# A four-layer graph network: nodes dealt to partitions in fours, adjacency alone on GpSimd's queue, and other work moved off GpSimd

**Chip, cores, metric.** One core of one Trainium2 chip. The metric is the device time of a run in microseconds (us); lower is better.

## The reference, cut to what matters

`x` is 8 x 2048 x 64, `adj` is 2048 x 2048 (random, symmetric in its zeros, each row scaled to sum 1). Every layer is pre-normed and added to `x`:

```python
# --- layer 0 (adj_preln) ---
h = jnp.maximum(_layernorm(x, axis=-1), 0.0)
x = x + _L0_gnn_ref(h, adj, embedding, weight, bias)    # h, A h, 2 A A h - h; weights per node
# --- layer 1 ---
h = jnp.maximum(_layernorm(x, axis=-1), 0.0)
x = x + _L1_gnn_ref(h, adj, ...)                        # three steps, each with one adj @ v
# --- layer 2 ---
h = jnp.maximum(_layernorm(x, axis=-1), 0.0)
x = x + _L2_gnn_ref(h, adj, ...)                        # one adj @ x
# --- layer 3 ---
h = jnp.maximum(_layernorm(x, axis=-1), 0.0)
x = x + _L3_gnn_ref(h, adj, a)                          # attention
return x
```

## The kernel before

The kernel keeps the signs of the whole adjacency on chip (`BT`, 8 MB as fp32) and scales the sums of each product by a row factor (`crow`). In the prologue, TensorE forms seven of the eight first products while the sixteen adjacency chunks arrive; the eighth (its line is L494 before; below "the 7th bank is done" means the start of it) reuses a bank. Batches go in four pairs `p`, nodes in four blocks `nb` of 512. A float32 value is split into two parts, `H` (a rounded copy by ScalarE) and `L` (the rest, by VectorE), and each part is multiplied.

Names in the lines below: Pool is GpSimd's short name in the profile. `bv_..a` and `bv_..b` are layer 0's first and second products; in layer 0 `y` is the product with the per-node weights and `odd` half of its sums on VectorE; `ph` belongs to layer 1, `e` is layer 2's product, `pS` and the other `y` are layer 3's sums and the row made of them. `h` is the normed `x`, `hb` a block of it that was stored and is loaded again. `MD` is the copy of the transposed signs in the chip's large memory (DRAM).

The places that the change and the argument touch:

```python
def fill_x(acc, layer, p, nb, queue=nc.sync):           # x of one block: runs of 64 floats, 256 B
    if layer == 0:
        for bb in range(2):
            ld = queue.dma_start(
                acc[:, :, bb * C:(bb + 1) * C],
                x[2 * p + bb].rearrange("(j p) c -> p j c", p=P)[:, part(nb), :],
            )
        return ld
# ... (cut)
def load_adj(m):                                        # one chunk: 128 rows of 8 KB, on Pool's queue
    loads.append(nc.gpsimd.dma_start(BT[:, m, :], adj[m * P:(m + 1) * P, :]))
# ... prologue: Pool issues chunks of adj between loads of x (lx) and powers (cut)
pool_loads(order[0], ((row, 0), (lx, 2), (row, 1), (lx, 3), (row, 2)))
plan = {
    0: (0, ((lx, 4),)), 1: (1, ((row, 3), (lx, 5), (row, 4))),
    2: (2, ((lx, 6), (row, 5), (lx, 7))), 3: (3, ((row, 6), (row, 7), (dia, 0), (dia, 1))),
    # ... (cut)
}
# ... layer 0, after each block's sums (cut)
nc.vector.tensor_tensor(acc, acc, odd, op=ALU.add)
keep(p, nb, acc, f"1_{p}_{nb}")     # starts the norm, stores the sums to xs (Pool queue);
                                    # the store of h (Pool queue) follows when the norm is done
# ... then, in the block loop (cut)
with tc.issue_after(kept[-1].ins):
    m = 4 * p + nb
    nc.gpsimd.dma_start(MD[m * P:(m + 1) * P, :], BTf[:, m, :])   # fp32 -> bf16 on the way
# ... layer 1, last step (cut)
acc = load_x(1, p, nb)
nc.gpsimd.tensor_tensor(acc, acc, rows4(b2r), op=ALU.add)
pn = back_to_nodes(g_new[nb], w2T, nm)
nc.vector.tensor_tensor(acc, pn, acc, op=ALU.add)
# ... layer 3, the end (cut)
for nb in range(NB):
    acc = accs[NB * p + nb]
    (nc.gpsimd if nb == 0 else nc.vector).tensor_tensor(acc, acc, rows4(y), op=ALU.add)
    queue = (nc.gpsimd, nc.sync, nc.scalar, nc.sync)[nb] if p == NP - 1 else nc.sync
    for bb in range(2):
        queue.dma_start(
            out[2 * p + bb].rearrange("(j p) c -> p j c", p=P)[:, part(nb), :],
            acc[:, :, bb * C:(bb + 1) * C],
        )
```

## Time and profile before

| kernel before | value |
|---|---|
| median of three runs | 1280.3 us (1279.38 to 1283.99) |
| span of the profiled run | 1278.6 us |
| TensorE busy | 1217.3 us, 95% |
| first matmul | 15.1 us |
| 7th bank done (first matmul of L494) | 81.5 us |
| last `y` of layer 3 (start of its making; behind it only adds and stores) | 1261.9 us |
| from there to the end of the span | 16.8 us |

### The profile page before, as it was taken

The numbers are of one execution on the slowest core, as the hardware profiler recorded it, in microseconds if no ns is written. First come the engines' busy times: TensorE is split into PE (matmuls) and PEld (weight loads), VectorE is DVE, ScalarE is ACT, GpSimd is POOL, SyncE is SP. The second block draws the span as 40 slices with busy tenths as digits, with TensorE's granted clock in tenths as the row PEclk, the third lists the DMA queues.
The fourth block names the chain that finished last, engine by engine and source line by source line (L and its number), as shares of the span: only waits on it lengthen the run. The fifth ranks groups of instructions, "written<-read, shape, count | busy, mean of one in ns | idle before, by whom it ended". The sixth has DMA issues, their size and how long they took to land.

```text
span 1278.6 us, 15515 instructions
## 1 busy us (share of the span) xinstructions
PE 1217.3 (95%) x5702; PEld 862.7 (67%) x5702; DVE 751.4 (59%) x1936; ACT 182.3 (14%) x281; POOL 236.8 (19%) x244
## 2 busy tenths in 40 slices
PE   4899999999999999999999999999999999999993
PEld 3665554555575556755567888787788787788882
DVE  5445887767746776377654446445543554575653
ACT  5530010000010000000011121112111111211100
POOL 6410211111121111011110024004102400432222
PEclk9999999999999999999999999999999999999996
DMA  8982343323332222122255425433643543524321
GB/s 265 343 208 74 96 112 87 90 70 84 95 105 71 71 79 66 65 62 62 67 141 136 102 93 158 112 92 121 150 117 87 159 116 86 161 95 115 108 58 36
DMA packets 140057, 141.14 MB, mean 110 GB/s; under 512 B 95093, under 2 KB 97141, under 8 KB 137925
## 3 DMA queue, kind: packets, MB, share of 16 engines
q1 hardware_dynamic: 121092, 82.05, 25.2%
q0 software_dynamic: 12160, 49.10, 12.8%
q10 hardware_dynamic: 6720, 8.92, 2.5%
q8 instruction: 47, 0.77, 0.2%
q14 instruction: 38, 0.30, 0.1%
HBM read 95.92 MB, written 35.73 MB: 103 GB/s over the span
## 4 chain that ended last, share of the span: by engine, by line
PE 83%; DMA 6%; DVE 4%; issue 3%; POOL 2%; ACT 1%; SPq 0%; ACTq 0%; POOLq 0%; DVEq 0%
PE bv L222 34%; PE y L632 23%; PE bn L587 4%; PE ph L804 3%; PE bv_0b L222 2%; PE bv_2b L222 2%; DMA BT<-in_adj_dram 2%; PE bv_3b L222 2%; PE bv_1b L222 2%; DMA hb<-hs 1%; POOL rstd L170 1%; PE bv_0a L222 1%; PE bv_3a L222 1%; PE bv_2a L222 1%; PE bv_1a L222 1%
## 5 line engine op out<-in xcount | busy, mean ns | idle before, releaser
L222 PE MATMUL bv<-BT,H 128*128 128x512 f32 x1024 | 426.7, 417 | 0.0
L222 PE MATMUL bv<-BT,L 128*128 128x512 f32 x1024 | 401.2, 392 | 0.0
L222 PEld LDWEIGHTS bv<-BT,H 128*128 128x128 f32 x1024 | 192.6, 188 | 47.9 <-issue 11.6
L222 PEld LDWEIGHTS bv<-BT,L 128*128 128x128 f32 x1024 | 192.9, 188 | 47.3 <-issue 11.5
L641 DVE SCALAR_TENSOR_TENSOR acc<-y,emb,acc 128x128 f32<-128x128 f32 x512 | 176.2, 344 | 65.8 <-PE y L632 62.4
L632 PE MATMUL y<-wt,t0T 64*128 64x512 f32 x512 | 144.2, 608 | 10.0 <-DVE odd L641 10.0
L641 DVE SCALAR_TENSOR_TENSOR odd<-y,emb,odd 128x128 f32<-128x128 f32 x448 | 153.3, 342 | 0.0
L170 POOL TENSOR_TENSOR rstd<-var,mhalf 128x8 f32<-128x8 f32 x64 | 107.9, 1688 | 194.5 <-DVE var L168 184.3
L214 DVE TENSOR_TENSOR g<-bv,crow 128x512 f32<-128x512 f32 x48 | 33.2, 691 | 183.7 <-PE bv L222 183.7
L164 ACT ACTIVATE sq<-z 128x512 f32<-128x512 f32 x64 | 40.4, 631 | 406.5 <-DVE z L160 397.4
L632 PEld LDWEIGHTS y<-wt,t0T 64*128 64x128 f32 x512 | 46.7, 187 | 73.9 <-issue 68.0
L612 POOL TENSOR_TENSOR acc<-acc,wl 128x512 f32<-128x512 f32 x16 | 20.6, 1289 | 297.3 <-DVE z L160 297.2
L613 POOL DMA_DIRECT2D xs<-acc x32 | 18.0, 562 | 276.2 <-DVE acc L649 254.2
L632 PE MATMUL y<-wt,t1T 64*128 64x512 f32 x256 | 67.9, 596 | 0.0
L173 DVE SCALAR_TENSOR_TENSOR z<-z,rstd 128x512 f32<-128x512 f32 x64 | 45.9, 723 | 28.2 <-POOL rstd L170 28.2
L587 PEld LDWEIGHTS bn<-wl,g 128*128 128x128 f32 x384 | 49.5, 191 | 6.3 <-ACT H L206 1.6
L167 DVE TENSOR_REDUCE var<-sq 128x8 f32<-128x512 f32 x64 | 43.5, 679 | 15.8 <-ACT sq L164 15.8
L587 PE MATMUL bn<-wl,g 128*128 128x128 f32 x384 | 51.1, 276 | 1.0 <-DVE var L168 0.5
L749 DVE SCALAR_TENSOR_TENSOR junk<-mt,cols,st 128x512 uint8<-128x512 bf16 x64 | 50.8, 794 | 0.6
L632 PEld LDWEIGHTS y<-wt,t1T 64*128 64x128 f32 x256 | 27.7, 188 | 27.3 <-issue 27.3
L809 ACT ACTIVATE g<-g,b1s 128x512 f32<-128x512 f32 x32 | 23.2, 724 | 139.4 <-DVE g L808 139.3
L160 DVE TENSOR_TENSOR z<-acc,mean 128x512 f32<-128x512 f32 x56 | 38.3, 690 | 6.6 <-DMA hs<-z 5.2
(209 smaller groups left out, 1677.3 us busy)
## 6 DMA issues: line engine op xcount, KB each, us to landing
BT<-in_adj_dram POOLq DMA_DIRECT2D x16, 1024.0 KB, 9.2
crow<-crowD SPq DMA_DIRECT2D x64, 256.0 KB, 3.2
st<-in_adj_dram SPq DMA_DIRECT2D x64, 256.0 KB, 3.4
hs<-z POOLq DMA_DIRECT2D x40, 256.0 KB, 2.8
xs<-acc POOLq DMA_DIRECT2D x32, 256.0 KB, 2.5
MD<-BT POOLq DMA_DIRECT2D x16, 512.0 KB, 5.0
acc<-xs SPq DMA_DIRECT2D x32, 256.0 KB, 3.2
hb<-hs SPq DMA_DIRECT2D x28, 256.0 KB, 3.6
```

What stands on the lines that cost most here:

```text
L160: firsts.append(nc.vector.tensor_tensor(g, groups(xt), mean[:, :, None].to_broadcast([P, 8, C]), op=ALU.subtract))
L164: squares.append(nc.scalar.activation(sq, z, AF.Square))
L167: nc.vector.tensor_reduce(var, groups(sq), axis=AX.X, op=ALU.add)
L170: powers.append(nc.gpsimd.tensor_tensor(rstd, var, mhalf, op=ALU.pow))
L173: nc.vector.scalar_tensor_tensor(groups(h), g, 0.0, rstd[:, :, None].to_broadcast([P, 8, C]), op0=ALU.max, op1=ALU.mult)
L214: ahead.append(nc.vector.tensor_tensor(out, ps, crow, op=ALU.mult))
L222: nc.tensor.matmul(ps, hl[m // 4][i][:, m % 4, :], BT[:, m, nb * 512:(nb + 1) * 512], start=(m == 0 and i == 0), stop=(m == NCH - 1 and i ...
L587: nc.tensor.matmul(ps[:, t, :], fT[:, t * P:(t + 1) * P], wmat, start=True, stop=True)
L632: nc.tensor.matmul(y[:, bb, :], terms[k][hs_, ts], wt[hs_, k, dg * 512:(dg + 1) * 512], start=(k == 0), stop=(k == K - 1),)
L641: last = nc.vector.scalar_tensor_tensor(xj, yd, ec, old, op0=ALU.mult, op1=ALU.add)
L749: nc.vector.scalar_tensor_tensor(junk, mt, cols[:, i, :], st, op0=ALU.mult, op1=ALU.not_equal, accum_out=bad[:, i, q:q + 1],)
L804: fill[12] = lambda: nc.tensor.matmul(ph, w1v2 if s else w1vT, gT[nb], start=True, stop=True)
```

## The change

Its intent: (1) a chunk of 128 rows holds every fourth node of a block, so that four neighbouring nodes lie in one partition and `x`, the embedding and the result move in runs of 1 KB instead of 256 B; (2) in the prologue `x` comes on SyncE's queue alone, Pool issues nothing but the adjacency, seven chunks at once, and ScalarE stores `h`; (3) the sums, whose columns are now nodes in another order, are read from PSUM in steps of four; (4) the constant `b2` is added in layer 0 instead of layer 1; (5) at the end all four adds are on VectorE and no store on Pool. The arithmetic is the same.

```diff
+    def rows_of(a, m):
+        return a.rearrange("(b p t) n -> b t p n", p=P, t=4)[m // 4, m % 4]
+    def runs_of(a, p, nb):
+        return a[2 * p:2 * p + 2].rearrange("e (b p t) c -> b p e (t c)", p=P, t=4)[nb]
 # fill_x
-            for bb in range(2):
-                ld = queue.dma_start(acc[:, :, bb * C:(bb + 1) * C], ...)      # cut
+            return queue.dma_start(runs(acc), runs_of(x, p, nb))
 # scaled (the sums)
-        ahead.append(nc.vector.tensor_tensor(out, ps, crow, op=ALU.mult))
+        crow, to = (a.rearrange("p (t q) -> p t q", t=4) for a in (crow, out))
+        ahead.append(nc.vector.tensor_tensor(
+            to, ps.rearrange("p (q t) -> p t q", t=4), crow, op=ALU.mult
+        ))
 # prologue
-    load_x01(nc.scalar)
-    load_x01()
+    for _ in norm_order:
+        load_x01(nc.sync)
-    pool_loads(order[0], ((row, 0), (lx, 2), (row, 1), (lx, 3), (row, 2)))
+    pool_loads(order[0], tuple((row, m) for m in range(7)))
+        1: (1, ((row, 7), (row, 8))), 2: (2, ((row, 9), (row, 10))),           # plan, cut
-        if m in (13, 14):                                                      # crow products
+        if m > 13:
-                for nb in (0, 1) if m == 13 else (2, 3):
+                for nb in (0, 1) if m == 14 else (2, 3):
 # layer 0 (keep) and layer 1
-        if more is not None:
-            nc.gpsimd.tensor_tensor(acc, acc, more, op=ALU.add)
+        nc.gpsimd.tensor_tensor(nodes(acc), nodes(acc), more, op=ALU.add)
-        keep(p, nb, acc, f"1_{p}_{nb}")
+        keep(p, nb, acc, f"1_{p}_{nb}", b2r[:, None, None].to_broadcast([P, 4, 2, C]))
-                    nc.gpsimd.tensor_tensor(acc, acc, rows4(b2r), op=ALU.add)
 # the end
-            (nc.gpsimd if nb == 0 else nc.vector).tensor_tensor(acc, acc, rows4(y), op=ALU.add)
-            queue = (nc.gpsimd, nc.sync, nc.scalar, nc.sync)[nb] if p == NP - 1 else nc.sync
+            nc.vector.tensor_tensor(nodes(acc), nodes(acc), rows4(y), op=ALU.add)
+            queue = nc.scalar if nb % 2 == 0 and p == NP - 1 else nc.sync
+            queue.dma_start(runs_of(out, p, nb), runs(acc))
 # cut: the prologue's stages of the norm in a stricter order, weight loads, embedding, diagonal
```

## The prediction

> **What bounds the kernel now.** I read first the page's busy shares and its 40 slices, then the table of stretches, the waits of the first 95 us, the order of work on Pool there, and the last 20 us in order of time.
>
> ```profile
> PE 1217.3 (95%) x5702; PEld 862.7 (67%) x5702; DVE 751.4 (59%) x1936; ACT 182.3 (14%) x281; POOL 236.8 (19%) x244
> ...
> PE   4899999999999999999999999999999999999993
> ...
> DMA  8982343323332222122255425433643543524321
> ```
>
> TensorE is full from the third slice to the last but one, so only the two ends can give much. The DMA row is high only in the first two slices. The table of stretches (stretch: length, PE, PEld, DVE, ACT, POOL busy, clock, DMA share, GB/s) confirms it:
>
> ```profile
> 0.00:10.00 10.00, 0.00 (x0) 0.00 (x0) 2.18 (x5) 1.72 (x2) 5.51 (x14) 1.00 0.87 261
> 10.00:20.00 10.00, 4.88 (x12) 3.83 (x13) 8.18 (x19) 7.97 (x11) 6.98 (x8) 1.00 0.88 266
> ...
> 30.00:40.00 10.00, 7.14 (x22) 4.92 (x23) 4.98 (x12) 4.55 (x6) 7.38 (x8) 0.85 0.92 308
> ...
> 60.00:70.00 10.00, 9.05 (x38) 6.68 (x37) 2.20 (x16) 6.13 (x7) 0.00 (x0) 1.00 1.28 416
> ...
> 300.00:700.00 400.00, 395.61 (x1807) 246.85 (x1804) 258.52 (x796) 32.82 (x55) 47.63 (x55) 1.00 0.32 83
> 700.00:1000.00 300.00, 299.00 (x1453) 240.81 (x1452) 143.25 (x265) 53.31 (x88) 53.93 (x50) 1.00 0.44 116
> ```
>
> From 300 to 1000 us TensorE lacks 5.4 of 700 us. The prologue moves 261 to 308 GB/s for 40 us, though the same engines reach 416 when only the adjacency is in flight. What waits there, in us in total, times, longest:
>
> ```profile
> PE bv_0a L418 <- ACT H L206: 15.1, 1, 15.1
> PE bv_0a L418 <- ACT BT L319: 4.5, 4, 1.9
> ...
> ACT BT L319 <- DMA BT<-in_adj_dram: 18.3, 10, 4.0
> ```
>
> The first matmul comes at 15.12 us, and afterwards the signs (and TensorE behind them) wait for adjacency rows. The rows come late because Pool issues them between other things. Its order of work (start, length, what):
>
> ```profile
> 5.90 0.59 POOL L305 DMA_DIRECT2D BT<-in_adj_dram  x1
> 12.02 3.29 POOL L170 TENSOR_TENSOR rstd<-var,mhalf 128x8 f32<-128x8 f32 x2 [5.53 <-DVE var L168]
> 15.27 1.55 POOL L126 DMA_DIRECT2D x<-in_x_dram  x2
> 16.81 0.57 POOL L305 DMA_DIRECT2D BT<-in_adj_dram  x1
> ```
>
> Three rows are out by 6.5 us and the fourth only at 16.8. The trace's single DMA packets show the hole: between 15.4 and 18.4 us no 8 KB adjacency packet starts at all.
>
> The end, in order of time:
>
> ```profile
> 1263.16 1.76 POOL L870 TENSOR_TENSOR acc<-acc,y 128x512 f32<-128x512 f32 x1 [4.19 <-DVE y L867]
> 1265.22 1.57 POOL L873 DMA_DIRECT2D out_dram<-acc  x2 [0.29 <-POOL acc L870]
> 1265.40 0.68 DVE L870 TENSOR_TENSOR acc<-acc,y 128x512 f32<-128x512 f32 x1
> ...
> 1266.11 1.24 SPq L873 DMA_DIRECT2D out_dram<-acc  x2
> ```
>
> The last store is issued by 1267.4, yet the span ends at 1278.6. The trace's raw records tell why: Pool waits until its own two stores have landed (1270.41), runs a semaphore step of 1.54 us, then a DRAIN of 5.62 us (1272.16 to 1277.78), and the other engines, done by 1273.4, wait for it.
>
> **What the Trainium skill says.** "DMA: Bandwidth & Descriptors", section Queues, rings and completion order: a DMA engine alternates between its queues at packet granularity. The trace agrees: with both queues full, from 4.5 to 5.5 us, 36 packets of 8 KB start beside 20 of 256 B, so a small packet waits for about one large one. The same page, Latency and other measured facts, has a large loss at row pitches of 512 KB and more; the new adjacency pitch is 32 KB, which no run here shows. "SBUF — State Buffer", Who interferes with whom: a VectorE instruction with two SBUF inputs and a GpSimd one that reads SBUF block each other. The trace agrees: the VectorE add beside Pool's took 1.75 us and the next 0.68. The same page, section Door 1, gives PSUM 8-byte lines and a penalty for broken access (stated for matmuls); no instruction before reads PSUM in steps, so this is open.
>
> **The change, part by part.**
>
> (1) Start. x now goes alone on SyncE, in 1 KB runs, one DMA per block. The first block used 1024 packets of 256 B on the ScalarE queue and was read at 7.92 us, its last packets stuck between adjacency packets. SyncE's first packets start at 1.9 us and Pool's at 3.7. Estimate: 16 packets of 1 KB per engine at about 0.055 us (the 2 KB h stores took 0.095) is 0.9 us, so two blocks pass before the adjacency starts; the first is usable near 4.5, 3.4 us sooner. The same chain of norm, power and copy then puts the first matmul at 11.5 instead of 15.1.
>
> (2) Stream. Seven rows are issued at once and the rest well ahead, so the DMA engines should never run dry. Work per engine: 128 adjacency packets at 0.35 us (between 0.328, alone, and 0.38, the mean) = 44.8; x, 93 packets left at 0.055 = 5.1; the diagonal, 16 of 4 KB at 0.2 = 3.2; h, 64 of 2 KB at 0.095 = 6.1. Sum 59.2, from 3.7: the last row ends near 63 where it ended at 70.5. Does x starve, alternating one to one? A round is about 0.42 us; 93 rounds put the eighth block at 44 us, and it is first needed with row 13, near 52. A pair of x blocks lasts four rows, and in 32 rounds exactly four rows arrive. It fits.
>
> (3) End of the prologue. The pass is 224 matmuls at 0.227 us = 50.9, plus some 2.4 for the slow clock of the first 5 us (0.43 per matmul) and 2.0 for the crow transposes: 55.3. From 11.5 that gives 66.8 as TensorE's floor. The DMA side gives 63 + 1 (landing) + 1 (half a sign) + 20 matmuls (4.5) + 1 = 70.5. The crow products move one row later, so the sums are scaled later and the next product may wait 1 us for its bank: 71.5, against 81.4 for the first matmul of L494 before. **Gain 10 us.**
>
> (4) The end. VectorE does four adds of 0.69 without Pool: 1263.1 to 1265.9; the last store is issued by 1266.4, in 1 KB runs, half as many DMAs. Pool's last work becomes the power ending 1259.0. With its branch, the 3.4 us it sat between branch and next step, 1.5 and 5.6 it is done near 1270. SyncE had 4.6 us from branch to next step and 1.4 of waits: 1266.5 + 6 = 1272.5, plus 0.7 for the last barriers: 1273.2. **Gain 5 us** (3 to 6).
>
> (5) Moved or hidden. 16 Pool adds of 1.29 us go from layer 1 to layer 0, where Pool idles hundreds of us. Sums read in steps of four: some 100 VectorE instructions of 0.69. If unchanged, nothing; if doubled, 70 us more on an engine at 59%, mostly beside products of 7.3 us: I allow 1 us in the mean. The weight loads become 3 + 3 copies on SBUF, ready near 72, wanted past 80. Fewer packets elsewhere: hidden.
>
> Sum: 1280.3 - 10 - 5 + 1 = **1266**.
>
> **Rivals.** (a) *The stream gains nothing*: total bytes do not fall and the DMA share was 0.9 already. For it: 16 engines at 0.9 for 70 us is most of what I sum up. If mixed packets take 0.40 (0.386 to 0.495 were seen in mixed stretches), the last row ends at 69 and the prologue gains 4: 1272. Against it: the hole on Pool, and 416 GB/s later. (b) *A new wait replaces the old*: the strict VectorE order, or an x block late between 8 KB packets, or the 32 KB pitch. Each would show as TensorE waiting for H or L; it would cost 5 to 10 us and leave about 1275. (c) *Stepped PSUM reads double* and the gap shows in layer 0, where TensorE already waits 10 us for VectorE: +3 to +8, about 1272. (d) *All works*: TensorE's floor of 67 is reached, the end gains 6, a clock dip (0.85 in 30 to 40) goes: 1260.
>
> **Range and chances.** My two gains are 4 to 14 and 3 to 6, the loss 0 to 5: 1258 to 1274. Over 2% means below 1254.7, past even (d): 0.07. Slower by 2% needs a pitch or starvation failure of 40 us: 0.02. Within 2%: 0.91.
>
> **What would show it.** Right: first matmul at 11 to 12; signs' wait for adjacency well below 18 us; no DMA hole in the first 60 us; L494 starting at 69 to 74; stepped reads still 0.69; nothing of Pool after 1260 but its DRAIN; last packet to end of span 3 to 5 us instead of 8. Wrong: 8 KB packets over 0.4 us (pitch, a); TensorE waiting for L or H (b); stepped reads over 1 us (c); or Pool's DRAIN still ending last.

## The result, and the profile after

The changed kernel took 1263.26 us (median of 4 runs, 1260.85 to 1264.67), the kernel before in the same rounds 1281.19. The ratio is 0.9856, 95% interval 0.9829 to 0.9883: 1.4% less, within the 2% that counts as the same. All ratios here are the mean time of one kernel's runs over that of the kernel before's runs of the same rounds, so not quite the ratio of the medians quoted. The median of the kernel before moved between 1277.8 and 1281.2, which is why the ratio matters more than the time. All outputs are right.

The page after: busy shares, then TensorE's and the DMA engines' busy tenths in 40 slices.

```profile
PE 1214.6 (96%) x5702; PEld 862.1 (68%) x5702; DVE 745.8 (59%) x1940; ACT 182.2 (14%) x281; POOL 218.6 (17%) x225
...
PE   5989999889999999999999999999999999999995
...
DMA  9951343123332132222246625433653563433311
```

TensorE does the same 5702 matmuls in nearly the same busy time; its first slice is a little fuller. But the 3rd, 8th and 9th slices have an 8 that was a 9 before: something got worse near 64 to 96 and 221 to 284 us. The table of stretches after (stretch: length, PE, PEld, DVE, ACT, POOL busy, clock, DMA share, GB/s):

```profile
0.00:10.00 10.00, 0.00 (x0) 0.00 (x0) 5.28 (x12) 2.54 (x3) 6.83 (x16) 1.00 0.74 221
10.00:20.00 10.00, 7.34 (x21) 5.82 (x22) 5.53 (x11) 7.93 (x10) 4.96 (x6) 1.00 1.07 406
...
30.00:40.00 10.00, 9.52 (x42) 7.53 (x41) 5.30 (x11) 5.95 (x8) 4.90 (x5) 1.00 1.07 408
...
60.00:70.00 10.00, 9.59 (x47) 7.22 (x46) 3.03 (x5) 3.84 (x4) 1.04 (x2) 1.00 0.83 144
```

From 10 to 40 us the DMA engines move some 407 GB/s where they moved 266 to 308, and by the seventh stretch they are nearly done. The waits of the first 95 us after (total, times, longest), and Pool's order of work (start, length, what):

```profile
PE bv_0a L462 <- ACT H L230: 12.7, 1, 12.7
...
ACT BT L348 <- DMA BT<-in_adj_dram: 8.7, 7, 2.7
```

```profile
1.48 3.92 POOL L334 DMA_DIRECT2D BT<-in_adj_dram  x7 [0.17 <-issue]
7.82 3.28 POOL L194 TENSOR_TENSOR rstd<-var,mhalf 128x8 f32<-128x8 f32 x2 [2.42 <-DVE var L191]
11.06 1.14 POOL L334 DMA_DIRECT2D BT<-in_adj_dram  x2
```

Seven chunks are out by 5.4 us, nine by 12.2. In the single packets no pause of over half a us is left between the starts of adjacency packets (before: six such places, the longest 15.4 to 18.4 us).

The sums of the products as VectorE reads them from PSUM: the group of instructions before (first fence, plain) and after (second, in steps of four); the columns are count, busy us and mean ns, then the idle time ahead and what ended it.

```profile
L214 DVE TENSOR_TENSOR g<-bv,crow 128x512 f32<-128x512 f32 x48 | 33.2, 691 | 183.7 <-PE bv L222 183.7
```

```profile
L240 DVE TENSOR_TENSOR g<-bv,crow 128x512 f32<-128x512 f32 x48 | 33.2, 691 | 183.2 <-PE bv L250 183.2
```

Not one ns is lost. The end of the span after, in order of time:

```profile
1253.96 2.50 DVE L921 TENSOR_TENSOR acc<-acc,y 128x512 f32<-128x512 f32 x4
1254.69 1.59 ACTq L923 DMA_DIRECT2D out_dram<-acc  x2
1255.28 2.37 SPq L923 DMA_DIRECT2D out_dram<-acc  x2
```

The last store is issued by 1257.7 and the span ends at 1262.9.

A milestone's gain is how much earlier it comes than in the kernel before; it accumulates.

| milestone, us | before | after | gain so far |
|---|---|---|---|
| first matmul | 15.12 | 12.66 | 2.5 |
| 7th bank done | 81.49 | 71.24 | 10.3 |
| first product behind it (`bv_0b`) | 94.58 | 86.38 | 8.2 |
| layer 1's first products (`ph`) | 658.08 | 653.33 | 4.8 |
| first sums of layer 3 (`pS`) | 1131.48 | 1123.95 | 7.5 |
| last `y` | 1261.87 | 1252.71 | 9.2 |
| end of span | 1278.63 | 1262.88 | 15.8 |

So the prologue gave 10.3, of which 2.1 were lost at the transition behind it and 3.5 more in layer 0; 4.4 came back in layers 1 to 3, and the end gave 6.6.

**Where layer 0 lost it.** The single largest wait of TensorE in layer 0 is that for VectorE's sums (`odd`). Total us, times and longest, 100 to 660 us, before, then after:

```profile
PE y L632 <- DVE odd L641: 10.0, 7, 2.9
```

```profile
PE y L687 <- DVE odd L696: 14.4, 7, 5.4
```

And one place where it happens, in order of time: Pool's stores, the load of `h` (`hb`), and ScalarE's rounding of it. Before:

```profile
223.53 0.55 POOL L708 DMA_DIRECT2D MD<-BT  x1
227.81 0.33 ACTq L136 DMA_DIRECT2D hb<-hs  x1
231.61 0.62 ACT L206 CAST H<-hb 128x512 fp32r<-128x512 f32 x1 [2.37 <-DMA hb<-hs]
```

After:

```profile
212.66 1.67 POOL L668 TENSOR_TENSOR acc<-acc,b2r 128x512 f32<-128x512 f32 x1 [17.12 <-DVE z L181]
214.63 0.56 POOL L669 DMA_DIRECT2D xs<-acc  x1 [0.30 <-POOL acc L668]
215.18 0.54 POOL L763 DMA_DIRECT2D MD<-BT  x1
215.58 0.33 ACTq L150 DMA_DIRECT2D hb<-hs  x1
222.66 0.62 ACT L230 CAST H<-hb 128x512 fp32r<-128x512 f32 x1 [5.65 <-DMA hb<-hs]
```

The Pool add that came over from layer 1 stands ahead of the stores of the sums and of `MD` (the transposed signs), which therefore go out later. Before, the store of `MD`, which takes 5.0 us in the median from issue to landing, was issued 4.3 us before the load of `hb`; after, 0.4 us before it, and the load, which took 3.8 us at this place before, takes 7. VectorE's order is strict: it waits for the rounding, and TensorE waits for VectorE.

**The end in the raw records** (not a view of the profile; start and length in us of the closing steps). A semaphore step of Pool (INC) and its DRAIN came last before and are long over after:

```
before  Pool INC 1270.58 1.54   Pool DRAIN 1272.16 5.62   SyncE's last DRAIN 1273.44   end 1278.63
after   Pool INC 1251.72 0.61   Pool DRAIN 1252.35 1.78   SyncE's last DRAIN 1261.97   end 1262.88
```

### The profile page after: what moved, and what is told of

Its sections match the earlier page's. It is cut to its first block, busy times and chain, and to the rows that moved or that the text cites. A ratio compares the mean times of both kernels' runs of the same rounds, so it can differ in the third digit from the quotient of the medians.

```text
span 1262.9 us, 15351 instructions
## 1 busy us (share of the span) xinstructions
PE 1214.6 (96%) x5702; PEld 862.1 (68%) x5702; DVE 745.8 (59%) x1940; ACT 182.2 (14%) x281; POOL 218.6 (17%) x225
## 4 chain that ended last, share of the span: by engine, by line
PE 86%; DMA 6%; DVE 3%; issue 2%; SPq 1%; POOL 0%; ACT 0%; POOLq 0%; DVEq 0%; ACTq 0%
PE bv L250 37%; PE y L687 23%; PE bn L641 5%; DMA emb<-in_L_gnn_embedding_dram 4%; PE ph L855 3%; PE bv_0b L250 2%; PE bv_2b L250 2%; PE bv_3b L250 2%; PE bv_1b L250 2%; PE bn_u L641 1%; PE bv_0a L250 1%; PE bv_3a L250 1%; PE bv_2a L250 1%; PE pS L904 1%; PE bv_1a L250 1%
## 5 line engine op out<-in xcount | busy, mean ns | idle before, releaser
L250 PEld LDWEIGHTS bv<-BT,L 128*128 128x128 f32 x1024 | 192.7, 188 | 47.5 <-issue 11.5
L668 POOL TENSOR_TENSOR acc<-acc,b2r 128x512 f32<-128x512 f32 x16 | 22.4, 1397 | 327.9 <-DVE z L181 327.9
L801 DVE SCALAR_TENSOR_TENSOR junk<-mt,cols,st 128x512 uint8<-128x512 bf16 x64 | 47.7, 745 | 3.7 <-DMA mt<-MD 3.2
L667 POOL DMA_DIRECT2D hs<-z x32 | 18.6, 582 | 144.9 <-DVE z L197 94.6
```

The source lines that it names most:

```text
L250: nc.tensor.matmul(ps, hl[m // 4][i][:, m % 4, :], BT[:, m, nb * 512:(nb + 1) * 512], start=(m == 0 and i == 0), stop=(m == NCH - 1 and i ...
L668: nc.gpsimd.tensor_tensor(nodes(acc), nodes(acc), more, op=ALU.add)
L801: nc.vector.scalar_tensor_tensor(junk, mt, cols[:, i, :], st, op0=ALU.mult, op1=ALU.not_equal, accum_out=bad[:, i, q:q + 1],)
```

## The experiments

My theory: the whole gain is the two ends, the prologue by a DMA stream without pauses (layout and schedule together), the end by Pool being out of the last stores; what was lost lies in the moved Pool add. Rivals: the layout alone or the schedule alone does it; the end is slow because of something other than the last stores; the loss in layer 0 is the old collision with `MD` and not the add.

### 1. The new schedule with the old layout

```diff
     def rows_of(a, m):
-        return a.rearrange("(b p t) n -> b t p n", p=P, t=4)[m // 4, m % 4]
+        return a[m * P:(m + 1) * P, :]
 # and x, the embedding, crow, the sums and the result in the old order, runs of 256 B
```

> The new kernel's schedule with chunks of consecutive nodes as before (x in 256 B runs on SyncE, rows 8 KB apart, sums read in order). My theory: the 1 KB runs are what makes the schedule possible, because a small x packet waits for one 8 KB adjacency packet. The third block then has 64 packets per engine instead of 16, at 0.345 + 0.03 us about 24 us, so it lands near 28 us instead of 12; the adjacency queue (nine rows) runs dry near 28 us, TensorE waits several us for H or L with row 4, and the first matmul of the seventh bank comes at 75 to 80 us instead of 71.2: total 4 to 8 us over the new kernel, near 1268. Rival A: the order on Pool alone made the gain and the run length does nothing: within 1 us of the new kernel. Rival B: reads in steps of four or a 32 KB pitch cost time: this one is faster than the new kernel.

Measured: 1278.37 us, ratio 0.9983 (0.9945 to 1.002): the same as before. The direction was right, the size under-estimated. The first matmul came at 28.0 us, later than in either kernel; the wait:

```profile
PE bv_0a L458 <- ACT H L235: 28.0, 1, 28.0
```

The second block of `x`, in 1024 runs of 256 B, advances about one run per 8 KB packet of the adjacency (from 15 to 16 us 51 such packets start beside 48 of 8 KB), and is read only at 22.3 us; VectorE's strict order has the second block's first stage ahead of the first block's last. The run has the changed end and the moved `b2` too: from the last `y` to the end it took 11.7 us instead of 16.8, while the 7th bank was done at 83.5, 2 us later than before. **What follows:** without the 1 KB runs the schedule gains nothing in the prologue, and the whole gains nothing clear of noise.

### 2. The new layout with the old schedule

```diff
 # kernel before, with rows_of, runs_of and the reads in steps of four; queues, plan and Pool's work as before
-    loads.append(nc.gpsimd.dma_start(BT[:, m, :], adj[m * P:(m + 1) * P, :]))
+    loads.append(nc.gpsimd.dma_start(BT[:, m, :], rows_of(adj, m)))
```

> The kernel before with the new chunks alone (1 KB runs of x and out, rows 32 KB apart, sums read in steps of four); order, queues, Pool's adds and last stores as before. With the run of old chunks under the new schedule it makes a square. Theory: x was on Pool's queue there, in series with the rows, and Pool's order set the prologue, so the layout alone gives 0 to 4 us (the first block lands sooner, the last stores are half as many): 1277 to 1281, and the seventh bank's first matmul at 78 to 82 us. Rival (the layout itself is the gain, whatever the order): the prologue ends near 71 to 73 us and the total is under 1272.

Measured: 1268.47 us, ratio 0.9907 (0.9865 to 0.9949), 7th bank done at 75.9. My expectation (0 to 4 us, 78 to 82) missed: the layout alone is worth 0.9% (10 us by the medians, 1278.56 for the kernel before). With experiment 1 this makes a square for the 7th bank: old layout and old schedule 81.5, old and new 83.5, new and old 75.9, new and new 71.2. **What follows:** the layout is worth 5.6 us of the prologue alone, and only on top of it the schedule is worth 4.7. The rival that the layout alone does it, which the prediction did not name, holds for about half of the gain; its figure for the 7th bank, 71 to 73, was not reached, its total under 1272 was.

### 3. Three chunks ahead instead of seven

```diff
-    pool_loads(order[0], tuple((row, m) for m in range(7)))
+    pool_loads(order[0], tuple((row, m) for m in range(3)))
-        1: (1, ((row, 7), (row, 8))),
+        1: (1, tuple((row, m) for m in range(3, 9))),
```

> The kernel after with three instead of seven adjacency rows issued at the start, the other four behind the second power on Pool. Theory A, that the gain of the prologue comes from a deep queue: a DMA hole opens after the third row (three rows of 1 MB at some 400 GB/s are moved by about 13 us, the fourth would be issued near 12 to 13 us), the last row ends 1 to 3 us later and the 7th bank starts at 72 to 74, total 1264 to 1267. Theory B, that 1 KB runs and Pool free of x are all of it: 7th bank at 71.2, total 1263.

Measured: 1264.99 us, ratio 0.9893 (0.9864 to 0.9923). Theory A fell: no pause between adjacency packets, 7th bank done at 70.2. Pool issued the other six chunks from 11.0 us, and with `x` in the stream as well the first three were still being moved. The median is 1.7 us over the changed kernel's, inside the spread. In the profiled run the transition (from the 7th bank to `bv_0b`) took 19.4 us instead of 15.1: there VectorE sat 5.2 us behind a small weight load (`wnl`) ahead of it in its order. **What follows:** a depth of seven is not needed; three chunks last until Pool, free of `x`, comes back.

### 4. Only the end changed

```diff
 # kernel before, and:
-            (nc.gpsimd if nb == 0 else nc.vector).tensor_tensor(acc, acc, rows4(y), op=ALU.add)
-            queue = (nc.gpsimd, nc.sync, nc.scalar, nc.sync)[nb] if p == NP - 1 else nc.sync
+            nc.vector.tensor_tensor(acc, acc, rows4(y), op=ALU.add)
+            queue = nc.scalar if nb % 2 == 0 and p == NP - 1 else nc.sync
```

> The kernel before with the end alone: last stores on ScalarE and SyncE, all adds of y on VectorE. Theory: two gains, about 5 us in the tail (from y to the end 16.8 before, 11.7 in the run of old chunks under the new schedule) and 2 to 3 us in layer 2, where VectorE was held up beside Pool's adds and TensorE waited 2.5 us for e: total 7 us less, about 1273.5. Rival 1: the tail gains only what 1 KB runs give, under 2 us. Rival 2: the hold-ups in layer 2 cost nothing, so layer 2 takes as long as before.

Measured: 1276.67 us, ratio 0.9972 (0.9929 to 1.0015). From the last `y` to the end: 11.9 instead of 16.8, so the end is worth 4.9 by itself. In the whole no gain is shown, and the second part of the theory, 2 to 3 us in layer 2, fell: the last `y` came 2.0 us later, at 1263.9. TensorE's wait for `e` at the start of layer 2 was longer, 3.5 us instead of 1.3 at that place, with a stretch of 3.4 us at half the granted clock behind it, both as in experiment 2, and there was a new wait of 3.4 us in layer 0 (`y` for `t2T_0b`). Experiments 2 and 4 still have the Pool add in layer 1; the changed kernel has no wait for `e`. Pool's DRAIN was still 5.45 us, but beside the last stores.

### 5. One last store back on Pool, in 1 KB runs

```diff
-            queue = nc.scalar if nb % 2 == 0 and p == NP - 1 else nc.sync
+            queue = (nc.gpsimd, nc.sync, nc.scalar, nc.sync)[nb] if p == NP - 1 else nc.sync
```

> The new kernel with one of the last four stores (block 0 of the last pair) back on Pool's queue, the adds all still on VectorE. Theory: Pool's closing DRAIN waits on its own store and comes after it, so the tail from the last y to the end grows from 8.9 us to 13 to 15 and the total by 4 to 6 us, to 1268. Rival: the tail gained from fewer and larger store packets and from VectorE not being held up: at most +1 us.

Measured: 1263.27 us, ratio 0.9858 (0.9821 to 0.9896); last `y` to end 10.7 instead of 10.2. Pool's DRAIN was 1.86 us. The theory that a last store on Pool makes the DRAIN long fell.

### 6. The same store on Pool, as 256 B runs

```diff
+            if nb == 0 and p == NP - 1:
+                for t in range(4):
+                    nc.gpsimd.dma_start(
+                        runs_of(out, p, nb)[:, :, t * C:(t + 1) * C],
+                        runs(acc)[:, :, t * C:(t + 1) * C],
+                    )
+            else:
                 queue.dma_start(runs_of(out, p, nb), runs(acc))
```

> The new kernel with one of the last four stores on Pool, in four DMAs of 256 B runs (1024 in all, as many as Pool's two had before). With 1 KB runs in one DMA Pool's DRAIN took 1.86 us and the time did not change, so my account of the tail fell in part. New theory: what made Pool's closing steps long (1.54 and 5.62 us) was the number of small packets that it had issued last; then the semaphore step is over 1.2 us, the DRAIN over 4 us, and the total 2 to 5 us over the new kernel. Rival: it was something else of the kernel before (its adds on Pool, its x loads from Pool): DRAIN at 1.8 to 2 us and under 1.5 us more in all.

Measured: 1266.66 us (1263.45 to 1268.1), ratio 0.9892 (0.9848 to 0.9935). DRAIN 2.11 us, not 5: the small last stores do not make it long either. In the profiled run they do cost: Pool's closing steps began only when they had landed, at 1261.6, and last `y` to end became 13.2 instead of 10.2. In the ratios the loss is not shown, as the intervals of this kernel and the changed one overlap.

### 7. Many small runs on Pool, none at the end

```diff
 # the eight later loads of x (pairs 2 and 3)
-        norm_relu(load_x(0, p, nb), f"0_{p}_{nb}", done)
+        acc = block("acc", f"acc_0_{p}_{nb}", 2)
+        for t in range(4):
+            nc.gpsimd.dma_start(
+                runs(acc)[:, :, t * C:(t + 1) * C],
+                runs_of(x, p, nb)[:, :, t * C:(t + 1) * C],
+            )
+        norm_relu(acc, f"0_{p}_{nb}", done)
```

> The kernel after with the eight later loads of x (pairs 2 and 3) issued by Pool in 256 B runs, four DMAs a block: 8192 small packets from Pool's queue, where the kernel before had 6144 of them. If the length of Pool's closing steps follows the small packets that Pool issued over the whole kernel, the semaphore step must be 1.5 to 2 us and the DRAIN 5.5 to 7.5 instead of 0.6 and 1.8, though no last store is on Pool. If it follows the last stores, they stay 0.6 and 1.8. The steps then lie beside the last stores, so the time is moved by at most 2 us either way.

Measured (one run, state unknown): 1264.58 us; INC 1.71 and DRAIN 6.27 us, starting at 1251.6, beside the last stores, so they cost nothing. This is what was expected of the theory of all runs. (The expectation calls them packets; the trace records Pool's queue in packets of 4 KB, each holding several runs, so "runs" is the right word.) Put in order by the runs of `x` and of the result that Pool issued in the whole kernel, worked out from the shapes (a block is 1024 runs of 256 B or 256 of 1 KB):

| kernel | such runs on Pool | DRAIN, us |
|---|---|---|
| after | 0 | 1.78 |
| 5, one store of 1 KB runs | 256 | 1.86 |
| 6, one store of 256 B runs | 1024 | 2.11 |
| 2, layout only | 1792 | 2.92 |
| 4, end only | 6144 | 5.45 |
| before | 7168 | 5.62 |
| 7, later loads of `x` | 8192 | 6.27 |

**What follows:** the DRAIN grows with the runs of `x` and of the result that Pool had issued, wherever in the kernel. Before, it was long mainly through the six blocks of `x` in the prologue, and it ended last because Pool's last stores made it start late.

### 8. `b2` added in layer 1 again

```diff
+        if more is not None:
             nc.gpsimd.tensor_tensor(nodes(acc), nodes(acc), more, op=ALU.add)
-        keep(p, nb, acc, f"1_{p}_{nb}", b2r[:, None, None].to_broadcast([P, 4, 2, C]))
+        keep(p, nb, acc, f"1_{p}_{nb}")
 # and in layer 1, behind load_x, the Pool add of b2r as before
```

> The new kernel with the b2 add back in layer 1 (16 Pool adds leave layer 0). Theory: in layer 0 the add delays the stores of acc and of the transposed signs by some 3.5 us, so that these collide with the load of h that VectorE's chain waits for; TensorE stood 5.4 and 3.3 us in the second pair's first two blocks, where before it stood 2.1 and 2.9. Without the add: both fall to about 2 to 3 us and the total to 1258 (1256 to 1260), less a few tenths lost in layer 1 where Pool's add holds up VectorE. Rival: the stalls were accidents of that one profile or of the earlier timing of everything: no change, 1263.

Measured: 1263.88 us (1259.29 to 1268.4), ratio 0.9879 (0.9838 to 0.992). In the total no gain is shown, as its runs spread over 9 us. The stretches of its profile tell more. From layer 1's first `ph` to layer 3's first `pS` it took 473.5 us, as the kernel before did (473.4), where the changed kernel took 470.6, and TensorE's wait for `e` was back, once, 1.7 us (2.5 before, none after). In all eight kernels that have the add in layer 0 (after and experiments 1, 3, 5, 6, 7, 9 and 11) this stretch took 470.4 to 470.6 us, in the five that have it in layer 1 (before and experiments 2, 4, 8 and 10) 473.2 to 477.2. Layer 0, from the first `bv_0b` to the first `ph`, was shorter here, 558.3 instead of 567.0. **What follows:** the move of the add is worth some 3 us in layers 1 and 2, and is suspected of the loss in layer 0.

### 9. The store of `MD` moved out of the way

```diff
-        norm_relu(acc, name, lambda z: nc.gpsimd.dma_start(hs[p][:, part(nb), :], z))
+        norm_relu(acc, name, lambda z: h_out.append(
+            nc.gpsimd.dma_start(hs[p][:, part(nb), :], z)
+        ))
 # node_weights, before the sums are added and kept
+        if h_out:
+            with tc.issue_after(h_out[-1].ins):
+                nc.gpsimd.dma_start(rows_of(MD, 4 * p + nb), BTf[:, 4 * p + nb, :])
         nc.vector.tensor_tensor(acc, acc, odd, op=ALU.add)
 # in the block loop
-            with tc.issue_after(kept[-1].ins):
+            if p + nb == 0:                        # only the first block as before
```

> The new kernel with the b2 add kept in layer 0, but the 512 KB store of the transposed signs issued before it, behind the h store in the middle of the block. Theory (the collision of that store with the load of h): as in e2, 1257 to 1260, and the load of h in the second pair's first blocks lands in under 4.5 us instead of 7. Rival (the Pool add holds VectorE up[...]): no gain, 1262 to 1264, with the stalls still over 3 us.

Measured: 1250.84 us (1249.77 to 1252.12), ratio 0.9767 (0.973 to 0.9804): faster than the kernel before, and whether by 2% is unclear, since the interval reaches past 0.98. The store cannot simply go to another queue: it turns float32 into bf16 on the way, and the Trainium skill, "DMA: Bandwidth & Descriptors", section SWDGE vs HWDGE vs iDMA, has casts during a DMA on GpSimd's queue alone (no run here tried it elsewhere). The same place as above, in order of time, and the wait for `odd`:

```profile
212.03 0.58 POOL L671 DMA_DIRECT2D xs<-acc  x1 [0.30 <-POOL acc L670]
...
212.99 0.33 ACTq L150 DMA_DIRECT2D hb<-hs  x1
...
216.58 0.62 ACT L230 CAST H<-hb 128x512 fp32r<-128x512 f32 x1 [2.17 <-DMA hb<-hs]
```

```profile
PE y L689 <- DVE odd L698: 6.3, 7, 1.9
```

The add on Pool is still there (it starts 2.0 us ahead of the `xs` store), the `MD` store is gone from this place, and ScalarE waits 2.17 us instead of 5.65. **What follows:** the collision with `MD`, not the add's own time, is the loss.

### 10. The same move in the kernel before

```diff
 # kernel before: h_out as in 9, and in node_weights
+        if h_out:
+            with tc.issue_after(h_out[-1].ins):
+                m = 4 * p + nb
+                nc.gpsimd.dma_start(MD[m * P:(m + 1) * P, :], BTf[:, m, :])
 # and the store in the block loop for p + nb == 0 alone
```

> The kernel before with one move only: the store of the transposed signs is issued behind the store of the middle block's h and so ahead of the store of the sums (seven of its eight per pass). If the collision of that store with the load of h is old and only made worse by the Pool add, the kernel before must gain too: its casts of h waited 2.4, 4.1, 2.1 and 3.9 us for that load where the fast kernel of this series waited 2.0 to 2.4, so about 4 us are there to win, with what VectorE makes of it some 3 to 6: 1274 to 1277 us. If the collision is only the Pool add's doing, nothing: 1279 to 1282.

Measured: 1271.35 us, ratio 0.9942 (0.9913 to 0.9971); the wait for `odd` 6.6 us. The gain is 6.4 us by the medians (1277.79 before), 0.58% by the ratio (0.29 to 0.87%); I had expected 3 to 6. The length of layer 0, from the first `bv_0b` to layer 1's first `ph`, in one profile each:

| | kernel before | kernel after |
|---|---|---|
| `MD` store as it was | 563.5 us | 567.0 us |
| `MD` store moved | 555.4 us | 555.6 us |

**What follows:** with the store out of the way both kernels have the same layer 0, though only one has the added Pool add there. So the collision is old, 8 us in the kernel before, 11.4 in the changed one; the 3.5 us that the change lost in layer 0 go away with it. How hard it hits depends on timing as well: with the store where it was, layer 0 took 558.3 to 565.0 us in the four kernels without the added Pool add (before and experiments 2, 4 and 8) and 565.0 to 567.7 in the six with it (after and experiments 1, 3, 5, 6 and 7). The two groups meet at their edges, so the add's share, 4.5 us between their means, is likely and not exact.

Not all of this is waiting. The traces also record stretches of 3.4 us (some of 6.8) in which TensorE was granted half its clock, and the kernels differ in how many. Layer 0 taken apart, in us, with half of the time at half clock counted as lost:

| kernel | layer 0 | TensorE's gaps (over 60 ns) | lost at half clock | rest |
|---|---|---|---|---|
| before | 563.5 | 12.7 | 5.1 | 545.7 |
| after | 567.0 | 15.1 | 6.7 | 545.2 |
| 8, `b2` back | 558.3 | 11.1 | 1.7 | 545.5 |
| 9, `MD` moved, after | 555.6 | 7.0 | 3.4 | 545.1 |
| 10, `MD` moved, before | 555.4 | 8.0 | 1.7 | 545.7 |

The rest is 544.0 to 545.9 in all thirteen kernels, so these two terms are the whole difference but for some 2 us. Of the 8 us that experiment 10 took from layer 0, 4.7 were gaps and 3.4 clock; of the 11.4 of experiment 9, 8.1 and 3.3; of the 3.5 lost by the change, 2.4 and 1.6. Of the 4.5 between the two groups, only 1.9 are gaps. That the waits bring the clock down is not shown: experiment 4 has 15.7 us of gaps and loses only 3.4 to the clock.

### 11. Experiment 9, and the crow products one chunk earlier

```diff
-        if m > 13:
+        if m in (13, 14):
             with tc.issue_after(last.ins):
-                for nb in (0, 1) if m == 14 else (2, 3):
+                for nb in (0, 1) if m == 13 else (2, 3):
```

> The new kernel with the store of the transposed signs moved to the middle of each block, as in the run before (1250.8), and the crow products one row earlier, after rows 13 and 14 as in the kernel before. Theory: the crow products after rows 14 and 15 leave VectorE behind at the end of the prologue, so that the time from the seventh bank's first matmul to the first product behind it is 13 to 15 us; earlier, it falls by 1 to 2 us and the total to 1249 (1248 to 1251). Rival: the products' own time moves ahead of TensorE's last row and costs there what it saves later: no change.

Measured: 1249.03 us (1248.1 to 1250.2), ratio 0.9759 (0.9718 to 0.9799). The transition from the 7th bank to `bv_0b` took 14.0 us (15.1 after, but 14.1 in experiment 9 too). Against experiment 9 the gain is 0.0008 in the ratio, less than the intervals, so the worth of this step is not shown. It is the fastest kernel of the study: 2.4% under the kernel before by the ratio, 1.1% under the changed one by the medians, which are of different calls.

## Why the prediction was right or wrong

The total was right: 1266 predicted, 1263.3 measured, inside 1258 to 1274, and the verdict within 2% as well. Part of it is luck, errors that nearly cancel. The range does not follow from its own parts either: gains of 4 to 14 and 3 to 6 and a loss of 0 to 5 would give 1260 to 1278.

**Start, right in kind.** The first matmul came at 12.7 instead of 11.5. `x` did come sooner (read at 3.7), but ScalarE signed the first adjacency chunk at 10.1 before it made `H`, which the chain of norm and power did not have in it.

**Stream, right.** Last adjacency packet at 61.5 (63 predicted), mean 0.337 us (0.35), no pause, `x` did not starve, the 32 KB pitch did no harm. The 7th bank done at 71.24 (71.5), gain 10.3 (10). What I did not see is that the layout is worth half of this under the old schedule too (experiment 2), and that the seven chunks are not needed (experiment 3).

**The products one chunk later.** The prediction put 1 us for them into its 71.5, as a wait of the eighth product for its bank, and nothing for the transition behind it, which grew by 2.1, from 13.1 to 15.1. It took 13.1 in all four kernels with the old schedule and 13.8 to 16.2 with the new one (19.4 in experiment 3). In experiment 11, with the crow products moved back, it was still 14.0, so they are not the whole of it. The traces show the larger part: TensorE's gaps in the transition grew from 1.6 to 3.4 us, and 1.3 of that are a wait for a copy (`bnb`) that stands in VectorE's order behind the small weight load `wnl`. In the four kernels with the old schedule VectorE came to `wnl` 19.8 us or more after the 7th bank, in the changed one 5.9 us after it, and had to wait 1.85 us for the load. A wait of TensorE for `L` fell from 0.7 to 0.2 us in experiment 11; no more than that can be put down to the crow products.

**The end, right in direction, the reason half wrong.** Predicted 5 (3 to 6), got 6.6. Experiment 4 puts the part that I reasoned out (Pool off the last add and stores) at 4.9, as predicted; the rest came by the layout, which alone is worth 4.1 (experiment 2: 12.7 instead of 16.8), so that the two overlap. But I took Pool's DRAIN for a fixed 5.6 us that would merely start sooner. It shrank to 1.78 since Pool issued fewer runs (experiment 7), which was not needed for the gain: at 6.27 it lay hidden too.

**Step (5), the failed one: the 16 adds called hidden.** I counted the time of the moved adds on Pool and found Pool idle, which is true, and did not ask what is queued behind them. In the trace they stand ahead of the `MD` store, which then meets the load of `hb`: the 3.5 us lost in layer 0, 2.4 of gaps and 1.6 of clock, are gone when that store is moved (experiments 9 and 10). I also missed what the move gives: in layers 1 to 3, 4.4 us came back. Its two waits for VectorE's `e`, at 1115 and 1181 us of the kernel before and 2.5 us in all, are gone, and from 700 to 1000 us TensorE is busy for all of the 300 (299.0 before):

```profile
700.00:1000.00 300.00, 300.00 (x1458) 241.59 (x1457) 142.29 (x268) 53.99 (x88) 43.91 (x43) 1.00 0.45 115
```

Experiment 8 puts 2.8 of the 4.4 down to the `b2` add (473.4 to 470.6 us, and 473.5 with the add put back). That an add on Pool holds up VectorE, as the prediction quotes of the Trainium skill for the last one, fits this: beside this add in the kernel before, VectorE's instruction at L749 took up to 1712 ns, against 744 in the median. The other 1.6 lie in layer 3, from the first `pS` to the last `y`: 130.4 us before, 128.8 after. Experiment 10 has the same layer 3 as the kernel before and took 129.1 (with no second wait for `e`), so most of that is the one profiled run and no gain of the change.

**Stepped reads.** Rival (c) fell: 691 ns as before. I had allowed 1 us and it cost none. Rivals (a) and (b) fell too; (d) comes nearest, though its floor of 67 was not reached.

In sum: +10.3 and +6.6 where I had 10 and 5, −2.1 at the transition and −3.5 in layer 0 where I had −1 in all, and +4.4 that I did not have, 2.8 of it shown: 15.8 in the profiled spans. In the medians it is 17.9; the difference is the spread between runs (the profiled run of the changed kernel, 1264.67, was the slowest of its four).

## What to carry to other kernels

When an instruction is moved to an idle engine, its own time is the small question; look at which transfers are queued behind it and what they will then meet. Here such a collision was in the kernel all along, cost 8 us of the profiled layer 0, and could be seen only as a small wait of an engine at 14%. And short runs that share the DMA engines with long packets can undo a better order of the queues (the 7th bank at 83.5 us with runs of 256 B, at 71.2 with 1 KB): make the runs longer first, then reorder the queues. Before a difference between two stages is put down to waits, take their clocks into account too.

## What the Trainium skill lacked or had wrong

- "PSUM — Partial Sum Buffer", and "SBUF — State Buffer", section Door 1: the 8-byte lines and the penalty are stated for matmuls, and nothing is said there of what reads in steps cost VectorE. In fp32, 128 x 512 multiplied from PSUM took 691 ns read plainly and 691 ns in steps of four.
- "DMA: Bandwidth & Descriptors", section Queues, rings and completion order, has the switching between queues but not its consequence for a kernel: a block of `x` in runs of 256 B that runs beside 8 KB packets held the first matmul until 28.0 us; in 1 KB runs it came at 12.7.
- The same page, section Latency and other measured facts, names pitches of 512 KB and more. A pitch of 32 KB did no harm: an 8 KB packet took 324 ns in the median and 337 in the mean, against 325 and 378 at a pitch of 8 KB in the kernel before, whose stream was mixed with more small packets.
- "VectorE: DVE Perf Modes", section The DRAIN you can't avoid, gives the DRAINs at a kernel's start and end a constant 12 ns or so on all five engines. Pool's closing one took 1.78 to 6.27 us here, growing with the runs of `x` and of the result that Pool had issued in the whole kernel (0 to 8192); no page has that growth.
- No page has how much a large store on GpSimd's queue delays a load on another queue: with a 512 KB store issued 0.4 us ahead, a 256 KB load took 7 us; at the same place without it, 3.6 to 4.3 (experiments 9 to 11).
